# A graph-attention layer and a graph convolution, each with residual and layer norm: the sorted table's rows fetched and weighted in two parts, row scaling and row adding apart, last store and two x loads at the seventh tile

## The chip, the cores and the metric

The kernel runs on one core of one Trainium2 chip. The metric is the device time of one execution in microseconds (us). The kernel before was run three times on the chip, and one further execution was recorded by the hardware profiler; its trace is what the readings below come from. A difference in the work of a slot counts about thirty times, because the kernel handles 32 images one after the other.

## The reference, cut to what matters

```python
def reference(x, adj, wq, wk, bm, bias):        # x (32, 512, 1024) f32, adj (512, 512) f32
    q = einsum('c,bcn->bn', wq, x); k = einsum('c,bcn->bn', wk, x)
    scores = leaky(q[:, None, :] + k[:, :, None])            # slope 0.01
    att = softmax(scores, axis=-1)                           # (b, m, n)
    agg = einsum('bcn,bmn->bcm', x, att)
    y = layernorm(x + relu(einsum('oc,bcm->bom', adj, agg) + bm[None, :, None]))
    W = adj * adj
    return layernorm(y + einsum('bnf,nm->bmf', y, W) + bias) # both norms over the last axis
```

A score depends only on the sum of one number of the source node (q) and one of the target node (k), and the leaky ReLU is linear on either side of zero. So the softmax-weighted sum over 1024 sources is a mix of a suffix sum and a prefix sum over the sources sorted by q. The kernel sorts, builds tables of running sums, and looks up the rows that a target needs.

## The kernel before, in words

**Tiles.** An image is 512 rows by 1024 nodes. `NT` = 8 tiles of 128 nodes, `CT` = 4 tiles of 128 rows. A projected row has `ZW` = 514 floats: q, 512 values, and k or 1.

**The path of one image.**

- `project` (L221) multiplies x by the transposed adjacency; an image takes 8 tiles in two parts each (`zp` in PSUM), copied by ScalarE to `zrow` (L229).
- `spread` broadcasts q over the partitions (`qb`, `qs`).
- `order` counts on VectorE for each node how many have a smaller q (`lt`, L262), and GpSimd scatters the rows to their ranks in a DRAM table `td` (L267, eight indirect DMAs). `count` does the like for k on ScalarE (L288).
- `fetch` waits for all eight scatters and reads the sorted rows back into `zs` through SyncE's queue: `NB` = 9 blocks of 120 rows, each in two halves of 60 partitions. Block 8 is the short last one (L315); blocks 0 to 3 and 4 to 7 follow in two DMAs each (L321).
- `weigh` makes exponential weights `w` of the fetched q column on ScalarE (L331, two instructions of 128x9) and spreads them over a triangle into `lw` on VectorE (L336, two of 128x576).
- `table(b, step)` (L351), nine steps, forms the running sums of block 8-step downward and of block step upward on TensorE (`tp`); ScalarE copies the result to `ts` (L356), then GpSimd (L360) and ScalarE (L362) copy the carry row into `zs` for the next step, and SyncE writes `ts` to `td` (L365). Step n+1 needs the carry of step n.
- `pick` gathers for each target the three rows that it needs into `g` (L379, eight indirect DMAs of GpSimd).
- `shares` makes the three mixing factors `ra`; `blend` scales a row by ScalarE (L410) and adds two scaled rows by VectorE (L412, two instructions a tile).
- `turn` transposes the mixed rows on TensorE (L447) with a ReLU on ScalarE (L451); `join` adds x on VectorE (L458) and takes the statistics (L421, L423); `root`, `shift`, `apply` finish the layer norm (GpSimd L429/L430, VectorE L436, ScalarE L441).
- `layer1` multiplies by the squared adjacency (L469, 64 matmul records an image, tile `o`), `stats1` adds the bias (L479), and the same norm steps end in `store` (L484).

**The order of work.** It is written out by hand: the program runs in a manual schedule, so each engine works through its instructions in the order in which the functions are called, and waits on semaphores where data or a buffer is missing. `begin` prepares two images, `slot(s)` is called for s = 0 to 29, and `end` finishes the last two. A slot advances three or four images at once: `new` = s+2 is projected, `mid` = s+1 has its table built, s gets `turn`, `join` and `layer1`, and `old` = s-1 has its last norm and stores.

Its first half is a loop over z = 0 to 7. TensorE runs `project(new, z, 0)`, a table step, `project(new, z, 1)`, a `turn` for z = 1 to 4, another table step. So table step 0 comes right after the first half of the first projection, step 1 after the second half, and step 8 at z = 4. `pick(mid)` follows at z = 4, `store(old, z)` at z = 0 to 3, x loads of image s+3 at z = 2 and 3 (first two row tiles) and at z = 5 (two more). Then `spread(new)`.

Its second half is a loop over h = 0 to 7 of `layer1`. `order` and `count` run at h = 0 to 2, `fetch(new)` is called at h = 3, `shares(mid)` at h = 4, `blend(mid, 0)` at h = 5, `weigh(new)` at h = 6, then `stats1(s, 2)`, `blend(mid, 1)` and two `apply` at h = 7. The next slot begins with the projection and the table steps.

SyncE's queue carries fetch, table writes, stores and x loads in call order. `zs` and `lw` have one buffer each, `g` one, `ts` two, x twelve tiles, the last norm's `v` four.

Of the kernel before, what the change touches and what calls it, by code (L numbers as in the profile page):

```python
# [8 lines left out]
F32 = mybir.dt.float32  # L9
# [14 lines left out]
def gat_gcn_resnorm_kernel(  # L24
# [39 lines left out]
    P = 128  # L64
# [244 lines left out]
    def fetch(b):  # L309

        zd = tds[b].rearrange("(s u) c -> s u c", u=3)
        for half in range(2):
            r = (NB - 1) * R + half * RH
            n = min(RH, N - r)
            nc.sync.dma_start(  # L315
                out=zs[half * G + 1 : half * G + 1 + n, NB - 1, :], in_=zd[r : r + n, 0, :]
            )
        zd = zd[0 : (NB - 1) * R, 0, :].rearrange("(j q p) c -> q p j c", q=2, p=RH)
        for j in (0, (NB - 1) // 2):
            for half in range(2):  # L320
                nc.sync.dma_start(  # L321
                    out=zs[half * G + 1 : half * G + 1 + RH, j : j + (NB - 1) // 2, :],
                    in_=zd[half, :, j : j + (NB - 1) // 2, :],
                )

    def weigh(b):

        bw = bws[b]
        w = small.tile([P, 2, NB], F32, name=f"w_{b}", tag="w")
        for i in range(2):  # L330
            nc.scalar.activation(  # L331
                w[:, i, :], zs[:, :, 0], AF.Exp, bias=bw[:, i : i + 1], scale=el[:, i : i + 1]
            )
        lt = junk.tile([P, 2, NB, G], F32, name=f"lw_{b}", tag="lw")
        for i in range(2):
            nc.vector.tensor_tensor(  # L336
                lt[:, i],
                tri[:, i, :].unsqueeze(1).to_broadcast([P, NB, G]),
                w[:, i, :].unsqueeze(2).to_broadcast([P, NB, G]),
                ALU.mult,  # L340
            )
        tabs[b] = lt

    def table(b, step):

        lt, td = tabs[b], tds[b].rearrange("(s w u) c -> s w u c", w=2, u=3)
        tp = ps_t.tile([P, 2, H], F32, name=f"tp_{b}_{step}", tag="t")
        js = (NB - 1 - step, step)
        for h in range(2):
            for i, j in enumerate(js):  # L350
                nc.tensor.matmul(  # L351
                    tp[i * G : (i + 1) * G, h, 0:CE], lt[:, i, j, :],
                    zs[:, j, h * CE : (h + 1) * CE], start=True, stop=True,
                )
        ts = tpool.tile([P, ZW], F32, name=f"ts_{b}_{step}", tag="ts")
        nc.scalar.copy(ts.rearrange("p (h c) -> p h c", h=2), tp[:, :, 0:CE])  # L356
        for i, j in enumerate(js):
            to = j - 1 + 2 * i
            if 0 <= to < NB and i == 0:
                nc.gpsimd.tensor_copy(zs[0:1, to, 1:ZW], ts[0:1, 1:ZW])  # L360
            elif 0 <= to < NB:
                nc.scalar.copy(zs[G : G + 1, to, 1:ZW], ts[G : G + 1, 1:ZW])  # L362
        for i, j in enumerate(js):
            n = RH if j < NB - 1 else TL
            nc.sync.dma_start(  # L365
                out=td[j * RH : j * RH + n, 0, 1 + i, :], in_=ts[i * G + 1 : i * G + 1 + n, :]
            )
# [34 lines left out]
        nc.vector.tensor_tensor(ra, ac, den.unsqueeze(2).to_broadcast([P, NT, 3]), ALU.mult)  # L402
        mixes[b] = (g, ra)

    def blend(b, h):

        g, ra = mixes[b]
        for k in range(h * (NT // 2), (h + 1) * (NT // 2)):
            u = g[:, k, 1, 1 : C + 1]
            nc.scalar.activation(u, u, AF.Copy, scale=ra[:, k, 1:2])  # L410
            for i in (2, 0):
                nc.vector.scalar_tensor_tensor(  # L412
                    u, g[:, k, i, 1 : C + 1], ra[:, k, i : i + 1], u, ALU.mult, ALU.add
                )
            us.setdefault(b, []).append(u)
# [70 lines left out]
    def begin():  # L486

        for z in range(NT):
            project(0, z, 0)
            project(0, z, 1)  # L490
        spread(0)
        for nt in range(NT):
            order(0, nt)
        top(0)
        fetch(0)
        for z in range(NT):
            project(1, z, 0)
            project(1, z, 1)
            count(0, z)
        share(0)  # L500
        weigh(0)
        spread(1)
        for step in range(NB):
            table(0, step)
            if step < NT:
                order(1, step)
        top(1)
        for mt in range(NT):
            pick(0, mt)
        fetch(1)  # L510
        bare(0)
        for nt in range(NT):
            count(1, nt)
        weigh(1)

    def slot(s):

        new, mid, old = s + 2, s + 1, s - 1
        tz, lz = (0, 1) if s > 0 else (1, 5)
        for z in range(NT):  # L520
            step, ot = 2 * (z - tz), z - lz
            project(new, z, 0)
            if 0 <= step < NB:
                table(mid, step)
            if 0 < ot < CT:
                root(0, s, ot - 1)
            if z == 0 and old >= 0:
                root(1, old, CT - 2)
            project(new, z, 1)
            if 0 < ot < CT:  # L530
                turn(s, ot)
            if 0 <= step + 1 < NB:
                table(mid, step + 1)
            if z == 0 and old >= 0:
                stats1(old, CT - 1)
                shift(1, old, CT - 2)
            if z == lz - 1 and old < 0:
                shares(s)
                for h in range(2):
                    blend(s, h)  # L540
            if ot == 0:
                turn(s, ot)
            if ot == CT - 1:
                for mt in range(3):
                    pick(mid, mt)
            if z == 1 and old >= 0:
                root(1, old, CT - 1)
            if 0 <= ot < CT:
                join(s, ot)
            if z == 1 and old >= 0:  # L550
                apply(1, old, CT - 2)
                shift(1, old, CT - 1)
            if ot == CT - 1:
                root(0, s, ot)
                for mt in range(3, NT):
                    pick(mid, mt)
            if ot == CT:
                shift(0, s, CT - 1)
                apply(0, s, CT - 1)
            if z == 2:  # L560
                if old >= 0:
                    apply(1, old, CT - 1)
                share(mid)
            if old >= 0 and z < CT:
                store(old, z)
            if new + 1 < B and ot in (1, 2):
                load(new + 1, ot - 1)
            if new + 1 < B and ot == CT:
                load(new + 1, 2)
                load(new + 1, 3)  # L570
        spread(new)
        if lz + CT >= NT:
            for ot in range(NT - lz, CT):
                root(0, s, ot - 1)
                turn(s, ot)
                join(s, ot)
            root(0, s, CT - 1)
            shift(0, s, CT - 1)
            apply(0, s, CT - 1)
            for mt in range(NT):  # L580
                pick(mid, mt)
            if new + 1 < B:
                for ct in (2, 3):
                    load(new + 1, ct)
        for h in range(CT * NH):
            layer1(s, h // NH, h % NH)
            if h < 3:
                for nt in range(3 * h, min(3 * h + 3, NT)):
                    order(new, nt)
                    count(new, nt)  # L590
            if h == 2:
                stats1(s, 0)
                root(1, s, 0)
                top(new)
            if h == 3:
                fetch(new)
            if h == 4:
                stats1(s, 1)
                root(1, s, 1)
                shares(mid)  # L600
            if h == 5:
                blend(mid, 0)
                shift(1, s, 0)
                shift(1, s, 1)
            if h == 6:
                bare(mid)
                weigh(new)
            if h == 7:
                stats1(s, 2)
                blend(mid, 1)  # L610
                apply(1, s, 0)
                apply(1, s, 1)

    def end():

        for s in (B - 2, B - 1):
            mid, old = s + 1, s - 1
            if mid < B:
                table(mid, 0)
            root(1, old, CT - 2)  # L620
            stats1(old, CT - 1)
            root(1, old, CT - 1)
            shift(1, old, CT - 2)
# [16 lines left out]
            for h in range(CT * NH):  # L640
# [12 lines left out]
                if h == 7:  # L653
                    stats1(s, CT - 2)
                    if mid < B:
                        shares(mid)
                        for half in range(2):
                            blend(mid, half)
        root(1, B - 1, CT - 2)
        shift(1, B - 1, CT - 2)  # L660
        apply(1, B - 1, CT - 2)
# [40 lines left out]
```

## Time and profile before

| what | value |
|---|---|
| median of the three runs (lowest to highest) | 2629.06 us (2628.16 to 2631.47) |
| the profiled execution's own time | 2626.74 us |
| its span, first to last instruction | 2625.0 us |
| TensorE busy (matmul) | 2386.5 us, 91% |
| VectorE, ScalarE, GpSimd busy | 61%, 55%, 39% |
| mean granted TensorE clock | 0.943 of full |
| DMA traffic | 548.63 MB, mean 209 GB/s |
| start of `layer1` in two slots in mid-kernel | 1125.41 and 1203.08 us |

Time outside the span is 1.74 us. The profiled execution lies 2.3 us below the median of the runs. The distance between two starts of `layer1` is one slot, 77.67 us here. From 351.28 to 2440.56 us there are 27 slots, 77.38 us each in the mean. TensorE's busy share includes work at a lower granted clock, so busy does not mean at full speed.

### The profile page before, as it was taken

To read this page: it belongs to the slowest core of one execution; us is meant where nothing else is said; L and a number is where in the kernel's file an instruction comes from. 1 tells how busy PE (TensorE), PEld (TensorE's weight loads), DVE (VectorE), ACT (ScalarE), POOL (GpSimd) and SP (SyncE) were. 2 spreads that over 40 slices of the span, in tenths; PEclk is the share of its full clock that TensorE was granted. 3 is DMA by queue.
4 is the path that set the end of the run, shared out by engine and by line. 5 is a ranking of instruction groups with operands and counts; after the bars stand their busy time and mean duration, and the time that the engine had idled before them with its cause. 6 is when DMAs were issued, how large, how long until landed. Compare 5 with 4: busy or idle time off the path is not lost.

```text
span 2625.0 us, 30494 instructions
## 1 busy us (share of the span) xinstructions
PE 2386.5 (91%) x9744; PEld 1481.0 (56%) x9744; DVE 1610.4 (61%) x3163; ACT 1454.3 (55%) x2147; POOL 1015.9 (39%) x1353
## 2 busy tenths in 40 slices
PE   8588999999999999999999999999999999999766
PEld 7354556665555666555666555566655566665422
DVE  3255666656766655766566676665576656567644
ACT  2454555665655665655566565556565556656432
POOL 1323444433443443344443344444334444334421
PEclk9689999999999999999999999999999999999887
DMA  6636667666667765667766666676666776666541
GB/s 234 180 132 205 215 231 251 226 207 188 215 226 230 245 224 184 206 210 235 245 228 210 189 212 225 228 242 226 193 201 208 230 249 228 209 196 205 183 159 48
DMA packets 175727, 548.63 MB, mean 209 GB/s; under 512 B 25328, under 2 KB 25328, under 8 KB 175568
## 3 DMA queue, kind: packets, MB, share of 16 engines
q1 hardware_dynamic: 116496, 276.65, 35.8%
q0 software_dynamic: 57344, 269.52, 27.1%
q8 instruction: 77, 1.26, 0.2%
q10 hardware_dynamic: 1728, 0.53, 0.1%
q14 instruction: 82, 0.67, 0.1%
HBM read 338.17 MB, written 208.43 MB: 208 GB/s over the span
## 4 chain that ended last, share of the span: by engine, by line
PE 62%; issue 16%; DVE 14%; POOL 4%; DMA 2%; ACT 2%; SPq 0%; POOLq 0%; ACTq 0%; DVEq 0%
PE zp L221 33%; PE o L469 13%; PE tp L351 11%; DVE lt L262 7%; PE op L447 4%; DVE st L421 2%; DVE v L479 2%; PE qb L237 1%; DVE g L412 1%; DMA g<-td,idx 1%; POOL zs L360 1%; DVE ranki L266 1%; POOL zs L372 1%; DVE qmax L281 1%; ACT qs L241 1%
## 5 line engine op out<-in xcount | busy, mean ns | idle before, releaser
L221 PE MATMUL zp<-wmT,x 128*128 128x257 f32 x4096 | 1007.5, 396 | 0.0
L469 PE MATMUL o<-y,adj_sb 128*128 128x512 f32 x2048 | 896.1, 598 | 16.5 <-ACT y L441 16.5
L221 PEld LDWEIGHTS zp<-wmT,x 128*128 128x128 f32 x4096 | 778.5, 196 | 223.0 <-issue 109.1
L469 PEld LDWEIGHTS o<-y,adj_sb 128*128 128x128 f32 x2048 | 390.3, 192 | 500.5 <-issue 467.9
L360 POOL COPY zs<-ts 1x513 f32<-1x513 f32 x256 | 206.2, 805 | 952.4 <-ACT ts L356 952.4
L351 PE MATMUL tp<-zs,lw 128*64 128x257 f32 x2304 | 369.2, 426 | 174.2 <-issue 127.3
L412 DVE SCALAR_TENSOR_TENSOR g<-g,ra 128x512 f32<-128x512 f32 x512 | 382.3, 778 | 34.3 <-ACT g L410 25.3
L379 POOL DMA_INDIRECT g<-td,idx x256 | 276.9, 1082 | 231.2 <-DMA x<-in_x_dram 113.1
L351 PEld LDWEIGHTS tp<-zs,lw 128*64 128x64 f32 x2304 | 162.9, 146 | 334.3 <-issue 202.0
L262 DVE SCALAR_TENSOR_TENSOR lt<-qs,zrow,first 128x1024 int8<-128x1024 f32 x256 | 327.1, 1278 | 27.5 <-ACT qs L241 27.5
L267 POOL DMA_INDIRECT td<-zrow,ranki x256 | 273.4, 1068 | 129.4 <-issue 65.3
L458 DVE TENSOR_TENSOR y<-y,x 128x1024 f32<-128x1024 f32 x128 | 156.8, 1225 | 257.4 <-ACT y L451 254.0
L288 ACT ACTIVATE sg<-qs,kc 128x1024 int8<-128x1024 f32 x256 | 293.9, 1148 | 8.0
L229 ACT COPY zrow<-zp 128x514 f32<-128x514 f32 x256 | 149.6, 586 | 188.7 <-PE zp L221 181.1
L356 ACT COPY ts<-tp 128x514 f32<-128x514 f32 x288 | 168.1, 584 | 150.5 <-PE tp L351 137.5
L441 ACT ACTIVATE y<-y,nb,rs 128x1024 f32<-128x1024 f32 x128 | 158.5, 1238 | 136.1 <-DVE nb L436 134.6
L436 DVE SCALAR_TENSOR_TENSOR nb<-mv,rs 128x1 f32<-128x1 f32 x256 | 35.2, 147 | 273.6 <-POOL rs L430 273.6
L441 ACT ACTIVATE v<-v,nb,rs 128x1024 f32<-128x1024 f32 x128 | 154.4, 1228 | 68.5 <-DVE nb L436 68.5
L410 ACT ACTIVATE g<-g,ra 128x512 f32<-128x512 f32 x256 | 163.2, 709 | 29.8 <-DVE ra L402 29.8
L429 POOL TENSOR_SCALAR rs<-mv 128x1 f32<-128x1 f32 x256 | 70.0, 273 | 263.2 <-DVE mv L423 216.4
L479 DVE TENSOR_TENSOR v<-o,bias_bc 128x1024 f32<-128x1024 f32 x128 | 156.0, 1219 | 25.3 <-PE o L469 25.0
L447 PE MATMUL op<-ident,g 128*128 128x128 f32 x1024 | 144.5, 284 | 25.8 <-DVE g L412 14.0
(68 smaller groups left out, 1436.2 us busy)
## 6 DMA issues: line engine op xcount, KB each, us to landing
x<-in_x_dram SPq DMA_DIRECT2D x128, 512.0 KB, 5.0
out_dram<-v SPq DMA_DIRECT2D x128, 512.0 KB, 2.9
zs<-td SPq DMA_DIRECT2D x128, 481.9 KB, 7.1
td<-ts SPq DMA_DIRECT2D x512, 120.5 KB, 2.0
td<-ts SPq DMA_DIRECT2D x64, 96.4 KB, 2.0
td<-zs SPq DMA_DIRECT2D x8, 514.0 KB, 9.0
td<-zrow,ranki POOLq DMA_INDIRECT x256, 6.9
g<-td,idx POOLq DMA_INDIRECT x256, 8.2
```

The costliest lines, as they stand in the source:

```text
L221: nc.tensor.matmul(zp[:, h, 0:CE], xb[ct][:, nt * P : (nt + 1) * P], wmT[:, ct, h * CE : (h + 1) * CE], start=(ct == 0), stop=(ct == CT - 1),)
L262: nc.vector.scalar_tensor_tensor(lt, qs, zrow[:, nt, 0:1], first[:, o : o + N], ALU.subtract, ALU.is_lt, accum_out=rank[:, nt : nt + 1],)
L267: sc = nc.gpsimd.indirect_dma_start(out=td[:, :], out_offset=bass.IndirectOffsetOnAxis(ap=ranki[:, nt : nt + 1], axis=0), in_=zrow[:, nt, ...
L288: nc.scalar.activation(sg, qs, AF.Sign, bias=kc[:, nt : nt + 1], accum_out=sgn[:, nt : nt + 1])
L351: nc.tensor.matmul(tp[i * G : (i + 1) * G, h, 0:CE], lt[:, i, j, :], zs[:, j, h * CE : (h + 1) * CE], start=True, stop=True,)
L360: nc.gpsimd.tensor_copy(zs[0:1, to, 1:ZW], ts[0:1, 1:ZW])
L379: nc.gpsimd.indirect_dma_start(out=gs[b][:, mt, :], out_offset=None, in_=tds[b].rearrange("(s u) c -> s (u c)", u=3), in_offset=bass.Indir ...
L412: nc.vector.scalar_tensor_tensor(u, g[:, k, i, 1 : C + 1], ra[:, k, i : i + 1], u, ALU.mult, ALU.add)
L441: nc.scalar.activation(t, t, AF.Identity, bias=nb, scale=rs)
L447: nc.tensor.transpose(op[:, mt * P : (mt + 1) * P], ub[mt][:, ot * P : (ot + 1) * P], ident)
L469: nc.tensor.matmul(op[:, h * H : (h + 1) * H], w1[:, ct, mt * P : (mt + 1) * P], yt[ct][:, h * H : (h + 1) * H], start=(ct == 0), stop=(ct ...
L479: nc.vector.tensor_tensor(t, ops.pop((b, mt)), bias_bc, ALU.add)
```

## The change

`fetch` reads the same bytes in eight DMAs instead of six. After the last block come blocks 0 and 1, then block 7, then blocks 2 to 6. `weigh` is cut in two calls. Part 0 makes the weights of blocks 7 and 8 downward and 0 and 1 upward, which table steps 0 and 1 read. Part 1 makes the rest; it is called in the next slot between table steps 0 and 1. `blend` is cut into `scale` (ScalarE) and `gain` (VectorE). In the slot the scaling stays where it was; of the additions, tiles 0 to 3 stay, tile 4 comes after `stats1(s, 2)`, and tiles 5 to 7 come in the next slot after the second part of the weights. The last `apply` of `old` moves from z = 2 to z = 6, its store from z = 3 to z = 6, and the last two x loads from z = 5 to z = 6, behind that store. `begin` calls both parts of `weigh` one after the other; `end` has the same moves as a slot.

```diff
     def fetch(b):
         zd = tds[b].rearrange("(s u) c -> s u c", u=3)
+        full = zd[0 : (NB - 1) * R, 0, :].rearrange("(j q p) c -> q p j c", q=2, p=RH)
         ...
-        for j in (0, (NB - 1) // 2):
+        for j0, j1 in ((0, 2), (NB - 2, NB - 1), (2, NB - 2)):
             for half in range(2):
                 nc.sync.dma_start(
-                    out=zs[half * G + 1 : half * G + 1 + RH, j : j + (NB - 1) // 2, :],
-                    in_=zd[half, :, j : j + (NB - 1) // 2, :],
+                    out=zs[half * G + 1 : half * G + 1 + RH, j0:j1, :],
+                    in_=full[half, :, j0:j1, :],
                 )
-    def weigh(b):
+    def weigh(b, part):
         ...
+        some = ((NB - 2, NB), (0, 2)) if part == 0 else ((0, NB - 2), (2, NB))
+        for i, (j0, j1) in enumerate(some):
             nc.scalar.activation(
-                w[:, i, :], zs[:, :, 0], AF.Exp, bias=bw[:, i : i + 1], scale=el[:, i : i + 1]
-            )
+                w[:, i, j0:j1], zs[:, j0:j1, 0], AF.Exp,
+                bias=bw[:, i : i + 1], scale=el[:, i : i + 1],
+            )
+        for i, (j0, j1) in enumerate(some):
             nc.vector.tensor_tensor(
-                lt[:, i],
+                lt[:, i, j0:j1],
         ...
-    def blend(b, h):
+    def scale(b, some):
         g, ra = mixes[b]
-        for k in range(h * (NT // 2), (h + 1) * (NT // 2)):
+        for k in some:
             u = g[:, k, 1, 1 : C + 1]
             nc.scalar.activation(u, u, AF.Copy, scale=ra[:, k, 1:2])
+
+    def gain(b, some):
+        g, ra = mixes[b]
+        for k in some:
+            u = g[:, k, 1, 1 : C + 1]
             for i in (2, 0):
                 nc.vector.scalar_tensor_tensor(...)
     def slot(s):
         ...
             if z == 0 and old >= 0:
                 root(1, old, CT - 2)
+                weigh(mid, 1)
+                gain(s, range(5, NT))
             project(new, z, 1)
         ...
             if z == 2:
-                if old >= 0:
-                    apply(1, old, CT - 1)
                 share(mid)
-            if old >= 0 and z < CT:
+            if old >= 0 and z < CT - 1:
                 store(old, z)
+            if old >= 0 and z == 6:
+                apply(1, old, CT - 1)
+                store(old, CT - 1)
         ...
-            if new + 1 < B and ot == CT:
+            if new + 1 < B and z == 6 and old >= 0:
                 load(new + 1, 2)
                 load(new + 1, 3)
         ...
             if h == 5:
-                blend(mid, 0)
+                scale(mid, range(NT // 2))
+                gain(mid, range(NT // 2))
                 shift(1, s, 0)
                 shift(1, s, 1)
             if h == 6:
                 bare(mid)
-                weigh(new)
+                weigh(new, 0)
             if h == 7:
-                stats1(s, 2)
-                blend(mid, 1)
+                scale(mid, range(NT // 2, NT))
                 apply(1, s, 0)
                 apply(1, s, 1)
+                stats1(s, 2)
+                gain(mid, [NT // 2])
```

More of the change, by code (lines that the diff above doesn't have):

```diff
@@ L317, in fetch @@
             )
-        zd = zd[0 : (NB - 1) * R, 0, :].rearrange("(j q p) c -> q p j c", q=2, p=RH)
-        for j in (0, (NB - 1) // 2):
+        for j0, j1 in ((0, 2), (NB - 2, NB - 1), (2, NB - 2)):
             for half in range(2):
                 nc.sync.dma_start(
-                    out=zs[half * G + 1 : half * G + 1 + RH, j : j + (NB - 1) // 2, :],
-                    in_=zd[half, :, j : j + (NB - 1) // 2, :],
+                    out=zs[half * G + 1 : half * G + 1 + RH, j0:j1, :],
+                    in_=full[half, :, j0:j1, :],
                 )
-    def weigh(b):
+    def weigh(b, part):
         bw = bws[b]
-        w = small.tile([P, 2, NB], F32, name=f"w_{b}", tag="w")
-        for i in range(2):
+        if part == 0:
+            w = small.tile([P, 2, NB], F32, name=f"w_{b}", tag="w")
+            lt = junk.tile([P, 2, NB, G], F32, name=f"lw_{b}", tag="lw")
+            tabs[b] = (lt, w)
+        lt, w = tabs[b]
+        some = ((NB - 2, NB), (0, 2)) if part == 0 else ((0, NB - 2), (2, NB))
+        for i, (j0, j1) in enumerate(some):
             nc.scalar.activation(
-                w[:, i, :], zs[:, :, 0], AF.Exp, bias=bw[:, i : i + 1], scale=el[:, i : i + 1]
-            )
-        lt = junk.tile([P, 2, NB, G], F32, name=f"lw_{b}", tag="lw")
-        for i in range(2):
+                w[:, i, j0:j1], zs[:, j0:j1, 0], AF.Exp,
+                bias=bw[:, i : i + 1], scale=el[:, i : i + 1],
+            )
+        for i, (j0, j1) in enumerate(some):
             nc.vector.tensor_tensor(
-                lt[:, i],
-                tri[:, i, :].unsqueeze(1).to_broadcast([P, NB, G]),
-                w[:, i, :].unsqueeze(2).to_broadcast([P, NB, G]),
+                lt[:, i, j0:j1],
+                tri[:, i, :].unsqueeze(1).to_broadcast([P, j1 - j0, G]),
+                w[:, i, j0:j1].unsqueeze(2).to_broadcast([P, j1 - j0, G]),
                 ALU.mult,
             )
-        tabs[b] = lt
     def table(b, step):
-        lt, td = tabs[b], tds[b].rearrange("(s w u) c -> s w u c", w=2, u=3)
+        lt, td = tabs[b][0], tds[b].rearrange("(s w u) c -> s w u c", w=2, u=3)
         tp = ps_t.tile([P, 2, H], F32, name=f"tp_{b}_{step}", tag="t")
@@ L500, in begin @@
         share(0)
-        weigh(0)
+        weigh(0, 0)
+        weigh(0, 1)
         spread(1)
@@ L513, in begin @@
             count(1, nt)
-        weigh(1)
+        weigh(1, 0)
+        weigh(1, 1)
     def slot(s):
@@ L538, in slot @@
                 shares(s)
-                for h in range(2):
-                    blend(s, h)
+                scale(s, range(NT))
+                gain(s, range(NT))
             if ot == 0:
@@ L619, in end @@
                 table(mid, 0)
+                weigh(mid, 1)
             root(1, old, CT - 2)
+            if mid < B:
+                gain(s, range(5, NT))
             stats1(old, CT - 1)
@@ L656, in end @@
                         shares(mid)
-                        for half in range(2):
-                            blend(mid, half)
+                        scale(mid, range(NT))
+                        gain(mid, range(NT))
         root(1, B - 1, CT - 2)
```

## The prediction

> **What bounds the kernel now.** I read the waits first, then the chain of waits over one slot, then the timeline around the one gap in it. TensorE is busy 91% of the span, so the question is what its other 9% wait for. The waits (engine, line, releaser: total us, times, longest):
>
> ```profile
> ACT w L331 <- DMA zs<-td: 234.7, 29, 14.7
> DVE lw L336 <- ACT w L331: 166.8, 32, 37.9
> PE tp L351 <- issue: 127.3, 31, 14.5
> PE tp L351 <- POOL zs L360: 43.3, 30, 6.6
> ```
>
> About once a slot TensorE stands before a table step, and before that VectorE stood for the weights and ScalarE for the fetch. The chain for one slot (start us, us, what) says where:
>
> ```profile
> 1125.57 27.47 PE o L469 x64
> 1153.04 1.74 PE zp L221 x8
> 1154.78 3.62 issue
> 1158.40 2.62 PE tp L351 x8
> 1161.01 3.41 PE zp L221 x8
> 1164.42 1.02 PE tp L351 x8
> 1165.44 1.94 PE zp L221 x8
> ```
>
> From 1164.42 on the slot is almost wholly TensorE at full speed; up to 1154.78 as well. Between them lie a gap of 3.62 us and two pieces that take 2.62 and 3.41 us where their like take 1.02 and 1.94: together 3.1 us lost to a slow clock (granted 0.50 from 1158.4 to 1161). The timeline tells what the gap waits for:
>
> ```profile
> 1144.81 0.69 SPq L315 DMA_DIRECT2D zs<-td  x2
> 1145.54 1.95 SPq L321 DMA_DIRECT2D zs<-td  x4
> 1157.10 0.69 ACT L331 ACTIVATE w<-zs,bw,el 128x9 f32<-128x9 f32 x2 [8.00 <-DMA zs<-td]
> 1157.54 1.43 DVE L336 TENSOR_TENSOR lw<-tri,w 128x576 f32<-128x576 f32 x2 [4.21 <-ACT w L331]
> 1157.70 2.55 ACT L410 ACTIVATE g<-g,ra 128x512 f32<-128x512 f32 x4
> 1160.15 2.36 ACT L441 ACTIVATE v<-v,nb,rs 128x1024 f32<-128x1024 f32 x2
> 1162.41 0.57 ACT L356 COPY ts<-tp 128x514 f32<-128x514 f32 x1
> 1163.05 1.15 POOL L360 COPY zs<-ts 1x513 f32<-1x513 f32 x1 [16.40 <-ACT ts L356]
> ```
>
> The weights wait for the whole fetch, 12.3 us after its first issue. After them ScalarE first works off scaling and two applies; only then does it copy table step 0 out, and step 1 starts on GpSimd's carry row (1163.05 + 1.15).
>
> Over slots 2 to 29 the gap is 2.2 to 4.84 us, 3.48 in the mean. From table step 0 to step 1 it takes 5.85 to 5.95 us, except in one slot, where full speed would give 1.02 + 1.94 = 2.96: 2.9 us more. **The prize is 6.4 us a slot.** Slot 1 has a gap of 10.66, slot 0 of 14.47, the end of 4.67 us.
>
> **What the Trainium skill says.**
>
> - "TensorE: Matmul & The Clock Gate", Part 1: an idle TensorE falls to half clock and needs about 3.4 us of work to return. The trace agrees (0.50 granted, 2.62 against 1.02 us); here 2.20 us of idling did it, and gaps of 1.1 us and less did not.
> - "DMA: Bandwidth & Descriptors", Queues, rings and completion order: an engine takes a ring's descriptors in order and shares itself among queues. So blocks asked for first come first, and x loads on SyncE's queue slow GpSimd's scatters. The trace agrees with the sharing (below); it shows no split fetch.
> - "SBUF — State Buffer", SBUF: two separate sides: VectorE and GpSimd contend for a port. The carry copy takes 1.15 to 1.18 us while VectorE adds rows and 0.61 after, so I use 1.15 for the carry of step 0.
>
> **The change, part by part.** Times are those of the slot above; TensorE is due at table step 0 at 1154.78.
>
> *Fetch in order of use.* The transfers run from 1145.5 to 1155.9 and bring 2.105 MB, 202 GB/s. The first part (block 8, blocks 0 and 1, block 7) is 0.131 + 0.493 + 0.247 = 0.871 MB, 4.3 us: data at 1149.8. From last data to the weights it took 1.2 us, and eight issues cost two more of 0.49 us, behind transfers: the first weights start at about 1151.2.
>
> *Weights part 0.* ScalarE has done its first four scalings by 1149.1 and is free. An `Exp` of 9 columns takes 395 ns; by the skill's "ScalarE: Activation LUTs", What ACT_TABLE_LOAD costs, a column is 0.833 ns on a fixed part, so 2 columns are estimated at 389: 0.69 us for two, to 1151.9. VectorE is busy with additions until 1153.2 and two `nb` until 1153.33; `lw` of 128x128 is priced by the row of that shape (285 ns), two make 0.57: 1153.9. **The gap of step 0 is gone**, with 0.9 us to spare, and with it the slow clock.
>
> *What is late next: step 1.* Scaling (2.55) and two applies (2.36) still stand between weights and copy-out: 1151.9 to 1156.8. `ts` 0.57, carry 1.15 and hand-overs of 0.1: step 1 can start at 1158.7. TensorE is ready at 1154.78 + 1.02 + 1.94 = 1157.74. A **new wait of about 0.9 us**, too short to cool the clock.
>
> *Weights part 1 and additions 5 to 7.* The two `Exp` (0.69 us) queue on ScalarE behind step 0's carry copy, in front of the `zrow` copy and step 1's copy-out; they wait for the rest of the fetch, ready at 1157.1 as now. ScalarE gets there at 1158.0, so the DMA does not hold it; `zrow` is out at 1159.3, before step 1 ends at 1159.7. Two `lw` of 448 columns take 0.62 us each (between the 128- and 576-column rows), done about 1160; step 2 is due at 1161.6. Six additions of 778 ns end near 1164.8; `turn` is due at 1165.7. VectorE's free 4.2 us before the weights hide `stats1(s, 2)` and tile 4. All of this at nothing; the cover is 1 us in places, and if the fetch slips it is gone.
>
> *Last apply, store and x loads to z = 6.* An apply of 1.23 us leaves a full stretch of ScalarE and now stands between the last two `zrow` copies. The `zrow` copy of z = 6 follows layer 0's last apply, which waits for GpSimd's `rs` behind three picks, and now runs 1200.51 to 1201.75. As it stands, `zrow` 7 would end near 1204.2 where TensorE needs it at about 1203: up to 1.3 us of delay a slot. But the picks wait for table writes that share SyncE's queue with these transfers:
>
> ```profile
> 1195.57 1.16 POOL L379 DMA_INDIRECT g<-td,idx  x1 [5.65 <-DMA x<-in_x_dram]
> ```
>
> A store (0.52 MB) and two loads (1.05 MB) less around them, at 230 GB/s (1190 to 1200), bring them 1 to 2 us forward, and most of the 1.3 is undone. I take 0.2 us lost, bounds 0 and 1.3.
>
> *The scatters.* The same 1.57 MB now runs beside picks and scatters, when the DMA is full (share 0.94 to 1.01, 360 to 419 GB/s from 1200 to 1220). 1.57 MB at 400 GB/s is 3.9 us; the loads of 1.05 MB overlapped that stretch in part before, and the picks start 1 to 2 us sooner. I take the fetch 0.3 us later, bounds -0.9 and +4. Every us that it slips costs a us at step 1, since weights, scaling, applies and copy-out follow in line.
>
> *Sum.* New loss a slot 0.9 + 0.3 + 0.2 = 1.4 us. 28 slots x (6.4 - 1.4) = 140; slot 1 about 6, slot 0 about 4 (its second weights still block ScalarE), end about 4: **154 us**. The profiled execution took 2626.74 us (span 2625.0 and 1.74 around it), which gives 2472; it lies 2.3 under the median of the runs, so 2629 - 154 = 2475.
>
> **The rivals.**
>
> - *Everything is hidden*: the picks come 2 us forward, the fetch with them by 0.9 us. Speaks for it: the last scatter is issued at 1141.39, 3.5 us after its rank (1137.85), because the picks stand before it on GpSimd. No loss remains: 28 x 6.4 + 14 = 193, **2436 us**.
> - *The fetch slips by 2 to 3 us* because picks don't come forward while loads collide with scatters. Loss 0.9 + 2.3 + 0.2 = 3.4: 28 x 3.0 + 8 = 92, **2537 us**.
> - *Slower.* The store and x loads stand in the rings during the scatters, and bytes are moved at the fetch's 206 GB/s, not at 400: 1.57 MB is 7.6 us. The fetch starts 7.6 us late, loss 0.9 + 7.6 = 8.5 against 6.4 won: 28 x 2.1 = 59 slower, **2688 us**. It decides from a slip of 5.5 us. Against it: with 512 KB loads in the mix the trace shows 400 GB/s and more.
> - *It doesn't do what it says*: TensorE's step 0 waits for all of `zs` all the same, or completions of the first part trail the second. Then nothing moves, **2629 us**. The instruction order shows step 0 waiting on the first part's DMAs alone.
>
> **How the numbers follow.** Likeliest case 0.50 (own range 2450 to 2505), all hidden 0.22, slip 0.18, slower 0.08, nothing 0.02. Faster sums to 0.90. A measurement of this kernel tells about 0.2% (5 us) from no change; little mass lies there, 0.02. The range 2434 to 2535 reaches from nothing lost to the fetch slipping some 2 us, and leaves out the slower cases.
>
> **What would show it right or wrong.** Right: slots of 71 to 73 us, the first weights within 7 us of the first fetch issue, no half clock in the slot, step 1 waiting under 1.5 us. Wrong: a gap before step 0 over 2 us with the clock at 0.50; fetch issues later than 21 us after `layer1` begins (19.4 now); TensorE waiting for `zrow` before `qb` over 1 us; ScalarE standing at the second weights.

## The result, and the profile after

The changed kernel takes **2497.31 us** (median of four runs, 2490.51 to 2505.88) against 2628.61 before (2623.79 to 2631.47): a ratio of 0.9504, 95% interval 0.9471 to 0.9537. The prediction was 2475 with a range of 2434 to 2535, so 131 us were won where 154 were forecast. The profiled execution took 2497.0 us (before 2626.74). The gap before table step 0 is gone. The wait before step 1, 0.44 us in the mean before, is now 1.72, where the prediction had 0.9, and 0.3 more for a later fetch.

The waits of the changed kernel (engine, line, releaser: total us, times, longest); L336 and L341 are now the weights, L355 the table matmul, L364 the carry row:

```profile
ACT w L336 <- DMA zs<-td: 126.6, 32, 11.9
DVE lw L341 <- ACT w L336: 100.9, 43, 29.0
PE tp L355 <- POOL zs L364: 88.5, 42, 10.8
PE tp L355 <- issue: 4.1, 2, 3.5
```

TensorE's 127.3 us ahead of step 0 have become 4.1, and its waits for the carry row have grown from 43.3 to 88.5. The timeline of the slot whose `layer1` begins at 1144.2 us shows how (start us, us, engine, line, what, idle before):

```profile
1165.26 0.69 SPq L316 DMA_DIRECT2D zs<-td  x2
1166.00 2.64 SPq L321 DMA_DIRECT2D zs<-td  x6
1171.47 0.67 ACT L336 ACTIVATE w<-zs,bw,el 128x2 f32<-128x2 f32 x2 [3.62 <-DMA zs<-td]
1171.99 0.49 DVE L341 TENSOR_TENSOR lw<-tri,w 128x128 f32<-128x128 f32 x2
1172.05 2.54 ACT L414 ACTIVATE g<-g,ra 128x512 f32<-128x512 f32 x4
1173.49 1.09 PE L355 MATMUL tp<-zs,lw 128*64 128x257 f32 x8
1174.50 2.36 ACT L451 ACTIVATE v<-v,nb,rs 128x1024 f32<-128x1024 f32 x2
1176.76 0.56 ACT L360 COPY ts<-tp 128x514 f32<-128x514 f32 x1
1177.39 0.60 POOL L364 COPY zs<-ts 1x513 f32<-1x513 f32 x1 [12.00 <-ACT ts L360]
1178.05 1.09 PE L355 MATMUL tp<-zs,lw 128*64 128x257 f32 x8 [1.54 <-POOL zs L364]
```

The first weights come 6.2 us after the first fetch issue, not 12.3, and step 0 runs at 1173.49 right behind the projection. Step 1 waits 1.54 us at the end of ScalarE's line: weights, four scalings, two applies, copy-out, then the carry.

All slots in the mean, from the timelines of each kernel (27 slots; fetch and weights counted from the start of the q copy `qs`, which runs 0.2 us after `layer1` begins):

| kernel | slot us | fetch starts | first weights | wait at step 0 | step 1 | step 2 |
|---|---|---|---|---|---|---|
| before | 77.38 | 18.28 | 31.34 | 3.46 | 0.44 | 0 |
| changed | 73.15 | 20.93 | 27.30 | 0 | 1.72 | 0 |

The slot fell by 4.23 us; 28 slots make 118 of the 130 us between the two profiled executions, and slots 0 and 1 with the end the rest. **The fetch starts 2.65 us later than before**, and that is where the missing time is.

In 9 of the 27 slots TensorE's clock fell to half after the wait at step 1. One of them (same columns; the granted clock was 0.65 and 0.63 of full in these two pieces):

```profile
740.20 1.58 PE L355 MATMUL tp<-zs,lw 128*64 128x257 f32 x8 [2.03 <-POOL zs L364]
741.71 3.15 PE L221 MATMUL zp<-wmT,x 128*128 128x257 f32 x8
```

against 1.09 and 2.01 us for the same pieces in the slot above. From step 1 to step 2 it took 3.49 us in the mean, 2.96 at full clock.

### The profile page after: what moved, and what is told of

Its sections match the earlier page's. It is cut to its first block, busy times and chain, and to the rows that moved or that the text cites. A ratio compares the mean times of both kernels' runs of the same rounds, so it can differ in the third digit from the quotient of the medians.

```text
span 2495.3 us, 30785 instructions
## 1 busy us (share of the span) xinstructions
PE 2329.1 (93%) x9744; PEld 1453.0 (58%) x9744; DVE 1614.4 (65%) x3227; ACT 1476.5 (59%) x2211; POOL 1024.8 (41%) x1353
## 4 chain that ended last, share of the span: by engine, by line
PE 51%; DVE 23%; issue 17%; POOL 4%; DMA 2%; ACT 2%; SPq 0%; POOLq 0%; ACTq 0%; DVEq 0%
PE zp L221 32%; DVE lt L262 11%; PE tp L355 11%; PE op L457 4%; DVE st L431 4%; DVE v L489 3%; PE o L479 3%; DVE g L422 1%; DVE ranki L266 1%; DVE qmax L281 1%; ACT qs L241 1%; DMA g<-td,idx 1%; POOL zs L376 1%; PE qb L237 1%; POOL rs L440 1%
## 5 line engine op out<-in xcount | busy, mean ns | idle before, releaser
L221 PE MATMUL zp<-wmT,x 128*128 128x257 f32 x4096 | 990.3, 391 | 0.0
L221 PEld LDWEIGHTS zp<-wmT,x 128*128 128x128 f32 x4096 | 766.0, 193 | 211.8 <-issue 81.6
L364 POOL COPY zs<-ts 1x513 f32<-1x513 f32 x256 | 203.4, 794 | 829.0 <-ACT ts L360 828.9
L355 PE MATMUL tp<-zs,lw 128*64 128x257 f32 x2304 | 332.9, 410 | 103.4 <-POOL zs L364 88.5
L267 POOL DMA_INDIRECT td<-zrow,ranki x256 | 298.5, 1166 | 202.2 <-issue 60.4
L383 POOL DMA_INDIRECT g<-td,idx x256 | 284.0, 1109 | 187.5 <-issue 121.4
L355 PEld LDWEIGHTS tp<-zs,lw 128*64 128x64 f32 x2304 | 147.9, 141 | 247.0 <-POOL zs L364 144.8
L431 DVE BATCH_NORM_STATS2 st<-v 128x6 f32<-128x512 f32 x256 | 164.7, 685 | 4.4
L431 DVE BATCH_NORM_STATS2 st<-y 128x6 f32<-128x512 f32 x256 | 164.7, 685 | 4.4
```

The lines of the kernel that those rows point to most:

```text
L221: nc.tensor.matmul(zp[:, h, 0:CE], xb[ct][:, nt * P : (nt + 1) * P], wmT[:, ct, h * CE : (h + 1) * CE], start=(ct == 0), stop=(ct == CT - 1),)
L267: sc = nc.gpsimd.indirect_dma_start(out=td[:, :], out_offset=bass.IndirectOffsetOnAxis(ap=ranki[:, nt : nt + 1], axis=0), in_=zrow[:, nt, ...
L355: nc.tensor.matmul(tp[i * G : (i + 1) * G, h, 0:CE], lt[:, i, j, :], zs[:, j, h * CE : (h + 1) * CE], start=True, stop=True,)
L383: nc.gpsimd.indirect_dma_start(out=gs[b][:, mt, :], out_offset=None, in_=tds[b].rearrange("(s u) c -> s (u c)", u=3), in_offset=bass.Indir ...
L431: nc.vector.bn_stats(st[:, h, :], t[:, h * H : (h + 1) * H])
```

## The experiments

My first theory was that the 1.57 MB of store and x loads, moved next to the picks and scatters, delay the fetch, and that ScalarE's line does the rest. The rival was that the shorter slot itself crowds the DMA.

**Only the split.** The kernel before with the new `fetch` and the two-part `weigh`; all else stays.

```diff
                 bare(mid)
-                weigh(new)
+                weigh(new, 0)
 ...
                 root(1, old, CT - 2)
+                weigh(mid, 1)
```

> The kernel before with only the fetch and the weights in two parts; additions, last apply, store and x loads stay where they were. Theory (the moved store and loads delay the fetch, ScalarE's line of scaling and two applies delays step 1, and the additions must make room for the second weights): the fetch starts about 18.3 us after the q copy as in the kernel before, step 0 has no gap, step 1 waits under 0.5 us, but the second weights queue behind eight additions on VectorE and step 2 waits 1 to 2 us, often with a cold clock: slots of 72.5 to 74 us, 2480 to 2520 us. Rival (the additions were never in the way): no wait at step 2, slots of about 71.2 us, 2440 us.

Measured: 2556.31 us, ratio 0.9734 (0.9708 to 0.9760). The fetch starts at 18.40 us, the first weights at 24.89, step 0 has no gap and step 1 waits 0.14 us. But step 2 waits 2.46 us:

```profile
PE tp L355 <- issue: 72.4, 31, 3.1
```

The slot takes 75.28 us. The mechanism is as the theory had it, and larger than its numbers: the time is 36 us above its range. From step 2 to step 3 it takes 4.69 us in the mean, not 2.96. In the five slots in which the clock stayed full after the wait it took 3.50, so about 1.2 us of these 1.7 are the slower clock. Compared with the kernel without moves below, which differs by the additions' place alone, moving the additions is worth 4.3 us a slot.

**Only the moves.** The kernel before with `apply(1, old, CT - 1)`, its store and the x loads at z = 6.

```diff
-                if old >= 0:
-                    apply(1, old, CT - 1)
                 share(mid)
-            if old >= 0 and z < CT:
+            if old >= 0 and z < CT - 1:
                 store(old, z)
+            if old >= 0 and z == 6:
+                apply(1, old, CT - 1)
+                store(old, CT - 1)
 ...
-            if new + 1 < B and ot == CT:
+            if new + 1 < B and z == 6 and old >= 0:
```

> The kernel before with only the last apply, its store and the last two x loads moved to the seventh tile. Theory (these 1.57 MB collide with picks and scatters): the fetch starts 20.5 to 21 us after the q copy instead of 18.3, and since the weights wait for all of it, the slot grows by as much, 2690 us in all. Rival (the fetch starts late in the changed kernel because its slot is shorter, the bytes a slot being the same): the fetch stays near 18.3 us and the time within 10 us of 2629 or under it.

Measured: **2698.78 us**, ratio 1.0264 (1.0234 to 1.0295). The fetch starts at 21.02 us, the slot takes 80.11: a slip of 2.74 and a slot longer by 2.73. The wait at step 0, over all slots, is

```profile
PE tp L351 <- issue: 207.1, 31, 14.9
```

where the kernel before had 127.3. The slot here is longer than before, so the rival falls.

**No moves.** The changed kernel with these steps back at their old places (the diff above, reversed).

> The changed kernel with the last apply, store and x loads back at their old places. Theory (the moves delay the fetch): the fetch starts 18.3 to 19 us after the q copy, the first weights at 25 to 26, step 1 waits 0 to 0.4 us instead of 1.72, no cold clock, slots of 71.2 to 71.6 us, 2440 to 2455 us. Rival (the shorter slot delays it): the fetch stays at 20.5 to 21 us, the picks come later again, and the time is 2497 us or more.

Measured: **2435.03 us**, ratio 0.9272 (0.9249 to 0.9296). The fetch starts at 18.35 us, the first weights at 24.83, step 1 waits 0.12 us, the mean slot takes 71.01 and most take 70.79. The chain of waits over such a slot is TensorE alone:

```profile
1187.65 27.47 PE o L479 x64
1215.12 1.74 PE zp L221 x8
1216.86 1.02 PE tp L355 x8
1217.88 1.94 PE zp L221 x8
1219.81 1.02 PE tp L355 x8
1220.83 1.94 PE zp L221 x8
```

So the moves cost about 62 us of what the rest of the change brings.

**Applies first.** The changed kernel, moves kept, with the two applies ahead of the weights, where ScalarE stands idle.

```diff
             if h == 5:
+                shift(1, s, 0)
+                shift(1, s, 1)
                 scale(mid, range(NT // 2))
+                apply(1, s, 0)
+                apply(1, s, 1)
                 gain(mid, range(NT // 2))
-                shift(1, s, 0)
-                shift(1, s, 1)
 ...
                 scale(mid, range(NT // 2, NT))
-                apply(1, s, 0)
-                apply(1, s, 1)
```

> The changed kernel with the two applies of v tiles 0 and 1, and the small VectorE step that they need, put ahead of the first weights, into the time in which ScalarE waits for the fetch. Theory (step 1 waits for ScalarE's line behind the first weights): the fetch stays at 20.9 us, the first weights at 27.3, step 1's wait falls from 1.72 us to 0.3 or less, no cold clock, slots of 71.2 to 71.6 us, 2440 to 2455 us. Rival (the wait is the fetch itself, or GpSimd's carry copy): the wait stays over 1 us and the time within 15 us of 2497.

Measured: 2461.95 us, ratio 0.9379 (0.9353 to 0.9405). Fetch at 20.91 and first weights at 27.17 us are as in the changed kernel; step 1's wait fell from 1.72 to 0.12 us. ScalarE's line is what step 1 waits for. The time is 7 us above my range: step 2 now waits 0.77 us, since the late fetch brings the second weights only at 33.24 us (31.75 without the moves). The slot takes 71.87 us.

**Which of the moved steps?** Two halves. With the store moved and the loads not:

```diff
-            if new + 1 < B and z == 6 and old >= 0:
+            if new + 1 < B and ot == CT:
                 load(new + 1, 2)
                 load(new + 1, 3)
```

> The changed kernel with the x loads back at z = 5; the last apply and store stay at z = 6. Theory (bytes beside the scatters delay the fetch, in proportion): 0.52 of 1.57 MB, so a third of the slip of 2.65 us: fetch 19.2 us after the q copy, step 1 waits about 0.4 us, slots of 71.3 us, 2440 to 2455 us. Rival (the x loads alone do it): fetch at 18.4, 2435 us as without any move.

Measured: 2436.08 us, ratio 0.9258 (0.9239 to 0.9276), fetch at 18.60 us, step 1 waits 0.07.

With the loads moved and the apply and store not:

```diff
-            if old >= 0 and z < CT - 1:
+            if old >= 0 and z < CT:
                 store(old, z)
-            if old >= 0 and z == 6:
-                apply(1, old, CT - 1)
-                store(old, CT - 1)
```

(`apply` is back at z = 2.)

> The changed kernel with the last apply and store back at their old places; the x loads stay at z = 6. Theory (bytes in proportion): 1.05 of 1.57 MB, two thirds of the slip: fetch at 20.1 us, step 1 waits about 1 us, slots near 72 us, 2460 to 2475 us. Rival (the store behind ScalarE's late apply does it): fetch at 18.4, 2435 us.

Measured: 2434.94 us, ratio 0.9259 (0.9244 to 0.9275), fetch at 18.37 us. **My theory of bytes in proportion failed here**: each half alone costs next to nothing, and together they cost 62 us. The reason stands in SyncE's own timeline, first of the changed kernel, then of the one with the store alone moved:

```profile
1130.76 0.75 SPq L369 DMA_DIRECT2D td<-ts  x2
1143.02 0.36 SPq L494 DMA_DIRECT2D out_dram<-v  x1
1143.47 0.99 SPq L155 DMA_DIRECT2D x<-in_x_dram  x2
1165.26 0.69 SPq L316 DMA_DIRECT2D zs<-td  x2
```

```profile
1106.80 0.75 SPq L369 DMA_DIRECT2D td<-ts  x2
1107.64 4.10 SPq L155 DMA_DIRECT2D x<-in_x_dram  x2
1119.07 0.34 SPq L494 DMA_DIRECT2D out_dram<-v  x1
1139.18 0.69 SPq L316 DMA_DIRECT2D zs<-td  x2
```

SyncE knows no z. It issues a load as soon as it comes to it and its tile is free. Written at z = 6 alone, the loads still follow directly on the last table write. What holds them is **the store in front of them, which waits for ScalarE's late apply**: from 1131.5 to 1143.02 the queue stands still, and the loads then run beside the scatters. The apply ends at 1143.00, and over the whole kernel the stores' waits for an apply (queue, line, releaser: total us, times, longest) are 425.9 us, against 93.6 before:

```profile
1141.76 1.24 ACT L451 ACTIVATE v<-v,nb,rs 128x1024 f32<-128x1024 f32 x1
SPq L494 <- ACT v L451: 425.9, 37, 26.8
SPq L484 <- ACT v L441: 93.6, 8, 26.5
```

In the mean the last load is issued 9.1 us before the q copy with the store alone moved and 0.3 us before it in the changed kernel. The last scatter goes out 13.8 us after the q copy in the one, 16.1 in the other.

**One load behind the store.** To see whether the held-back bytes set the slip, one load goes before the store and one stays behind it.

```diff
+            if new + 1 < B and z == 6 and old >= 0:
+                load(new + 1, 2)
             if old >= 0 and z == 6:
                 apply(1, old, CT - 1)
                 store(old, CT - 1)
 ...
             if new + 1 < B and z == 6 and old >= 0:
-                load(new + 1, 2)
                 load(new + 1, 3)
```

> The changed kernel with one of its two last x loads issued before the store of the seventh tile, the other still behind it, so that 0.52 MB of loads instead of 1.05 wait for ScalarE's late apply. Theory (in SyncE's queue the store's wait for the apply holds the loads behind it back into the stretch where picks and scatters fill the DMA, and the fetch slips with the bytes held back): the fetch starts at about 19.8 us after the q copy, halfway between 18.6 with no load behind and 20.9 with two; step 1 waits about 0.7 us, slots near 71.6 us, 2450 to 2465 us. Rival (the slip comes as a step, once any load is held back): fetch at 20.9, about 2497 us. Rival (one held-back load finds room): fetch at 18.6, 2436 us.

Measured: 2452.83 us, ratio 0.9330 (0.9314 to 0.9345), fetch at 19.81 us, step 1 waits 0.76, slots of 71.65 us. Fetch starts of 18.60, 19.81 and 20.93 us for none, one and two loads held back: 1.2 and 1.1 us for each load of 0.52 MB. All numbers of the theory were met, and both rivals fall. The store has 0.52 MB too and goes out 1.3 us before the q copy, 0.5 us ahead of this load, yet moved alone it delayed the fetch by only 0.25 us (18.35 to 18.60). Why a load costs so much more than the store is not shown.

**The order of the fetch alone.** The kernel without moves, with the old six DMAs; the weights stay in two parts.

```diff
-        for j0, j1 in ((0, 2), (NB - 2, NB - 1), (2, NB - 2)):
+        for j0, j1 in ((0, 4), (4, NB - 1)):
```

> The changed kernel without the moves and with the six fetch DMAs of the kernel before (blocks 0 to 3, then 4 to 7), the weights still in two parts. Theory (the order of the fetch opens step 0, not the split of the weights): the first weights need block 7 and wait for the whole fetch, 31.4 us after the q copy; step 0 has its gap of 3.5 us and the cold clock again, slots of 77 us, 2610 to 2640 us. Rival (smaller weights and moved additions bring a good part): 2550 us or less.

Measured: 2619.74 us, ratio 0.9963 (0.9943 to 0.9983). The gap is back:

```profile
ACT w L336 <- DMA zs<-td: 242.1, 29, 14.0
PE tp L355 <- issue: 120.4, 31, 14.5
```

Step 0 waits 3.30 us, step 1 another 1.21, and the slot takes 77.34. Without the order of the fetch, splitting the weights and moving the additions bring 0.4%.

**Both improvements.** No moves and the applies first.

> Both improvements at once: no moves (2435 us alone) and the two applies ahead of the first weights (2462 us with the moves). Theory: without the moves TensorE hardly waits in a slot (70.79 us of 71.01 in the mean), so only the few waits of 0.6 us at step 1 are left to win: 2427 to 2433 us. Rival: the applies take ScalarE from something that is on the path without the moves, and the time is over 2437 us.

Measured: **2432.29 us**, ratio 0.9254 (0.9241 to 0.9266). Step 1 waits 0.00 us and the slot takes 70.94. The interval overlaps that of the kernel without moves, so this version beats the changed kernel by 65 us, but whether the applies add anything without the moves is not resolved.

## Why the prediction was right or wrong, point by point

- **Step 0's gap goes: right.** First weights were forecast 6.4 us after the first fetch issue; 6.37 in the mean. Two `lw` took 0.49 us (0.57 forecast), two `Exp` 0.67 (0.69). The kernel with the old fetch order, whose first weights start 13.34 us after the first issue, shows that the gain rests on the order of the fetch. This agrees with what the Trainium skill's "DMA: Bandwidth & Descriptors" states (Queues, rings and completion order), that an engine takes the descriptors of a ring in order.
- **The prize of 6.4 us a slot: right in size, but half of it was put down to the wrong cause.** 77.38 less 70.79, the slot that the kernel without moves reaches, is 6.6. The prediction gave 3.1 us of the slot to the slow clock. But there is one slot before in which the granted clock stayed at 1.00 after the gap, and step 1 came no sooner:

```profile
1390.66 1.72 PE L351 MATMUL tp<-zs,lw 128*64 128x257 f32 x8 [2.80 <-issue]
1396.51 1.09 PE L351 MATMUL tp<-zs,lw 128*64 128x257 f32 x8 [2.19 <-POOL zs L360]
```

From step 0 to step 1 it took 5.85 us here, and 5.85 or 5.86 in the 15 other slots in which TensorE waited for the carry row. In the 12 slots without that wait, where the slow clock came last, it took up to 6.27 us (the prediction read 5.85 to 5.95 in all slots but one); the mean of all is 5.95. So step 1 waited before, too, for ScalarE's line behind the weights, and the slow clock added about 0.1 us a slot. The early weights end both, so the size held.
- **A wait at step 1 behind ScalarE's line: right in kind, 0.9 us and 0.3 for the fetch forecast, 1.72 measured.** Two terms were off, in opposite directions. From the first weights to step 1 it took 6.57 us in the mean, not 7.5 (1151.2 to 1158.7). The carry row took 0.60 us in all 27 slots, not 1.15: in the slot shown VectorE was waiting for the second weights (1.85 us) instead of adding rows, so that the contention for a port which "SBUF — State Buffer" (SBUF: two separate sides) describes did not arise. Most of the rest is that the prediction added whole durations, while each of ScalarE's instructions starts some 0.1 us before the one ahead of it ends (1172.05 + 2.54 is 1174.59, and the applies start at 1174.50). Against that, the fetch came 1.7 us later than in the one slot that the prediction read (20.93 against 19.2 from the q copy), not 0.3: 1.4 more. 0.9 + 0.3 + 1.4 - 0.9 = 1.7.
- **"I take the fetch 0.3 us later": the step that failed.** The mean slip is 2.65 us. The slot that it read had one of the latest fetches before (19.2 against 18.28 in the mean), which hid 0.9 of it. More important, the picks did come forward as said (the first from 8.17 to 9.70 us before the q copy), but that was no gain for the fetch. The first scatter came only 1.0 us sooner (2.99 us after the q copy, 4.01 without the moves), since VectorE has the first rank no sooner than at 2.53, and the last one went out 2.1 us later than without the moves. Crediting the earlier picks against the bytes was the error.
- **How the loads get beside the scatters: not seen.** I priced the loads' bytes but not that the store ahead of them makes them wait for an apply; the experiments show that this order, not the place in the loop, makes the collision.
- **"Too short to cool the clock": wrong in a third of the slots.** The prediction went by gaps of 1.1 us, which did not cool it, and of 2.20, which did; the slot shown above, where 2.80 and 2.19 us did not, was overlooked. In the changed kernel waits from 1.83 to 2.49 us cooled it in 9 slots, while 1.84, 1.89 and 2.03 us did not in three others. In the kernel with the old fetch order eight gaps before step 0 left it at full, the longest of them 3.43 us. So the length alone doesn't decide; what does is not shown. The extra is 3.49 - 2.96 = 0.53 us a slot. "TensorE: Matmul & The Clock Gate", Part 1, names an idle window of about 3.4 us; here 1.83 us was enough and 3.43 us was not.
- **Second weights, additions 5 to 7, `turn`: right.** Step 2 does not wait. The experiment with the split alone shows what it costs when the additions stay in front: 2.46 us and the slow clock.
- **The last apply between the `zrow` copies, 0.2 us: not seen.** TensorE never waited for `zrow` before `qb`, and from step 2 to the next `layer1` the slot takes 35.59 us, 35.65 without the moves. The slot is explained without it: 70.79 + 1.72 + 0.53 = 73.04 of 73.15. The first pick of the slot, which waited 5.65 us in the prediction's line, waits 3.32 us at its like in the changed kernel (at 1206.74), behind a table write.

- **The rivals.** "Everything is hidden" at 2436 us is what the change gives without its moves (2435.03). "The fetch slips by 2 to 3 us", to which the prediction gave 0.18, had the slip right (2.65 us) and the collision of loads with scatters, though not the picks, which did come forward. Its 2537 us is 40 too high, because it too has 0.9 us too much between the weights and step 1, and adds the slip to a slot whose fetch was late already. The slower case needed a slip of 5.5 us. "It doesn't do what it says" was not seen: step 0 has no gap.
- **In part luck.** The 22 us between 2475 and 2497 are less than the slip alone would have made: it was underrated by 1.4 us a slot, 39 us over 28 slots, and the overlong line to step 1 gave 0.9 of that back.
- **Its own signs.** Met: the first weights within 7 us of the first fetch issue (6.37), no gap before step 0. Not met: step 1 waiting under 1.5 us (1.72), no half clock in the slot (9 of 27 had it), slots of 71 to 73 us (73.15). One of the signs of being wrong came as well: the fetch starts 21.13 us after `layer1` begins, and 21 was the limit.

## What to carry to other kernels

Fetch first what is used first, and make the consumer wait for that part alone; here it bought 6.6 us a slot once the instructions in line behind it were out of the way. In an in-order DMA queue a transfer's place in the program is only its order: look at what each entry in front of it waits for, since a store that waits for a late engine moves every load behind it. When a transfer is shifted, check the stretch in which it then runs, and read start times over all slots, not from one. Before a cause is given its share of a gap, look for a slot in which it is absent: the slow clock was, once, and the gap stayed.

## What the runs showed of the hardware that was not expected

- 1.57 MB of store and loads collided only in a certain order of one queue: 18.60 us against 20.93 us for the start of the fetch, 2436 against 2497 us in all. A load of 0.52 MB held back beside the scatters cost the fetch 1.1 to 1.2 us, the store of the same size 0.25.
- TensorE's half clock came after idle times as short as 1.83 us and stayed away after 2.03 us in another slot of the same execution, and after 3.43 us in the kernel with the old fetch order. In the changed kernel it cost 1.3 to 1.7 us between step 1 and step 2 each time that it came; in the kernel before, where it came in all slots but one, it cost about 0.1 us a slot, since TensorE would have waited for the carry row anyway.
